# Four graph layers on one core: smaller diagonal tiles, one square per group and ten steps moved to ScalarE in the last layer

## The chip, the cores and the metric

The kernel runs on one core of one Trainium2 chip. The metric is device time in microseconds (us). The median of three runs of the kernel before is 1385.57 us, with 1384.66 us the lowest and 1387.64 us the highest. The engines are called by their names and by the short forms of the profile: TensorE (PE, with its weight loads PEld), VectorE (DVE), ScalarE (ACT), GpSimd (POOL) and SyncE (SP).

## The reference

The input is a matrix `x` of 4096 nodes by 64 features and a symmetric sparse adjacency matrix `adj` of 4096 by 4096. Four layers follow each other, each as `x = layernorm(x + layer(x, adj))`: a Chebyshev filter, a signed graph attention with a gated cell, a layer with decayed weights, and a hyperbolic layer. The change touches the last of them alone:

```python
def _mobius_add(x, y, c): ...
def _logmap(x, y, c):
    sub = _mobius_add(-x, y, c)
    sub_norm = jnp.maximum(jnp.linalg.norm(sub, axis=-1, keepdims=True), MIN_NORM)
    ...
    arg = jnp.clip(sqrt_c * sub_norm, 0.0, TANH_CLIP)
    return 2.0 / (sqrt_c * lam_x) * jnp.arctanh(arg) * sub / sub_norm

deg = jnp.maximum(adj.sum(axis=1, keepdims=True), 1e-08)
w = adj / deg
log_ij = _logmap(x[:, None, :], x[None, :, :], c)
agg = jnp.einsum('ij,ijc->ic', w, log_ij)
transformed = agg @ weight + bias
return _expmap(origin, transformed, c)
```

For each pair of nodes the kernel needs one scalar factor, an arctanh over its argument. It is a symmetric function of the pair, so the factor of a pair (i, j) serves (j, i) too. The kernel multiplies the adjacency matrix by the factors and then sums over the neighbours as matrix products.

## The kernel before, in words

The last layer goes over pairs of groups. A group is 512 nodes, four blocks of 128; there are eight groups, taken in the order `seq`. A tile is a pair of groups (i, j) with j not before i in `seq`: 36 tiles, in eight rows of 8, 7, 6, 5, 4, 3, 2 and 1 tiles. The first tile of each row is diagonal (i = j). A tile is worked on in two units of two blocks each, so there are 72 units; unit n belongs to tile n // 2, and `h` (0 or 1) is its half. An ordinary unit is 128 partitions by 2 x 512 = 1024 values. In a diagonal tile the first unit has the full 1024 values and the second unit only 2 x 256 = 512 (`columns`), because the lower left quarter of the tile is filled in by transposing the upper right one.

The chain of one unit is as follows.

- `product` (TensorE): two matrix products into the unit's PSUM tile `v_ps`. Unit n + 2 reuses the tile of unit n, so it waits for that unit's VectorE step at L1889.
- `square` (ScalarE, L1635): the square of the products, into `w3`.
- `opposite` (TensorE): a second pair of products added onto `v_ps`.
- `less_one` (VectorE, L1657): subtract a constant from the square and keep it above a floor (add, then max).
- ScalarE: logarithm of `w` (L1866), `exp(0.5 w)` into `rt` (L1867), `exp(-0.5 w)` (L1891), and later the logarithm of `rt` (L1900).
- VectorE: `rt = max(v, c) + rt` (L1889), and two units later the factor `f = min(rt, T_MAX) * w` (L1876) and `at = at * f` (L1879), the adjacency block times the factor.
- `turn` (TensorE transposes, L1678 and L1671): the factors of an off-diagonal tile are transposed for the mirrored tile, and VectorE multiplies the mirrored adjacency blocks (L1680, two per unit). In a diagonal tile four blocks are transposed and multiplied in (L1673), one iteration later than the factors themselves (`late_turns[n + 1]`).
- `gather` (TensorE, L1694 and L1706): the sums over the neighbours; ScalarE copies the mirrored part to `tb` (L1713).

The main loop runs one iteration per unit. The order of the main steps on ScalarE and on VectorE is fixed by hand: `behind(engine, ins)` ties each one to the one before it. In iteration n ScalarE does L1866(n), L1867(n), L1635(n + 1), L1891(n), a copy to `tb` in every second iteration, and L1900(n - 1). VectorE does L1876(n - 2), L1879(n - 2), L1889(n), L1657(n + 1), and two multiplications at L1680.

Other work is kept in a list of steps, `seam`; one step is taken at the end of each iteration. Its instructions are not tied, and the framework places them among the main ones. When a row of tiles is complete, six steps are added (`finals`): nothing, `first`, `second`, `third`, `fourth` and `fifth`, which turn the sums of a group into its output. `second` and `fourth` are mostly VectorE work, `third` takes the norm of each node with four squares on ScalarE that give their sums as well (L1808), followed by a maximum on VectorE (L1809) and small logarithms and exponentials on ScalarE (L1810 to L1812), and `fifth` is the layer norm. The last two groups are finished after the loop.

## Time and profile before

| what | value |
|---|---|
| median of three runs | 1385.57 us |
| profiled execution, its own time | 1386.67 us |
| its span, first to last instruction | 1384.9 us |
| granted TensorE clock, mean | 0.985 |
| PE busy | 1299.2 us (94%) |
| DVE busy | 1043.6 us (75%) |
| ACT busy | 810.5 us (59%) |
| first L1866 of the last layer | 958.62 us |
| last L1866 of the last layer | 1351.39 us |
| L1866, 128x1024, x64 from 880 us on | 1050 ns each |
| L1876, 128x1024, x64 from 880 us on | 1219 ns each |

The times come from one profiled execution. Its page gives the busy time of each engine, the span in 40 equal slices, and the costliest groups of instructions by source line. A group has the line, the engine, the operation, what it writes and reads, how often it ran, the busy time, the mean duration of one, and the idle time of the engine just before it with what ended that. "Busy" is an average over the four layers. The change is in the last layer, the last 430 us of the span, and it is read there.

### The profile page before, as it was taken

The page shows a single profiled execution, that of the slowest core. Times are in us where ns is not written, and L with a number is a line of the kernel's source. Part 1 is how long each engine was busy: PE and PEld are TensorE (multiplying, and loading weights), DVE is VectorE, ACT ScalarE, POOL GpSimd, SP SyncE. Part 2 cuts the span into 40 slices and gives each one's busy share as a digit, 9 for nine tenths or more (in the row PEclk, how much of TensorE's full clock was granted, in tenths as well). Part 3 has the DMA queues.
Part 4 walks back from the last instruction along what each step waited for, and adds up shares of the span by engine and source line. Part 5 has one row for each costly group of instructions (what it writes and reads, how often), then busy time and mean ns, then how long its engine had stood idle before and what let it go on. Part 6 is the DMA issues. An engine that isn't in the chain of part 4 may idle for free.

```text
span 1384.9 us, 19115 instructions
## 1 busy us (share of the span) xinstructions
PE 1299.2 (94%) x6812; PEld 613.3 (44%) x6812; DVE 1043.6 (75%) x1952; ACT 810.5 (59%) x1346; POOL 113.4 (8%) x200
## 2 busy tenths in 40 slices
PE   9999999999999999999999999998889898988984
PEld 6655656565544334444444323333334333433442
DVE  7789899899444257788885223335999999999997
ACT  5544444343000115654424775756989999999994
POOL 3111111101123000010111000001000000000000
PEclk9999999999999999999999999999999999999997
DMA  9999999999799999999985755443245453444430
GB/s 352 386 412 409 400 413 409 410 404 393 285 378 372 389 417 375 422 366 345 328 313 188 230 173 183 151 155 150 106 171 206 165 210 153 186 156 186 159 119 12
DMA packets 108191, 382.16 MB, mean 276 GB/s; under 512 B 20276, under 2 KB 20280, under 8 KB 76472
## 3 DMA queue, kind: packets, MB, share of 16 engines
q1 hardware_dynamic: 90472, 297.03, 57.8%
q0 software_dynamic: 12736, 76.29, 13.3%
q10 hardware_dynamic: 4880, 7.54, 1.4%
q8 instruction: 56, 0.92, 0.3%
q14 instruction: 47, 0.39, 0.1%
HBM read 294.05 MB, written 85.20 MB: 274 GB/s over the span
## 4 chain that ended last, share of the span: by engine, by line
PE 58%; ACT 17%; DVE 15%; DMA 6%; issue 3%; ACTq 0%; DVEq 0%; SPq 0%
PE pass L578 7%; PE tp L742 5%; PE w_ps L578 5%; DMA raw<-in_adj_dram 5%; PE cnt_ps L1506 4%; PE a_last L1215 4%; PE pass L571 4%; PE acc_ps L1466 4%; PE a_ps L1215 4%; ACT rt L1867 3%; ACT w L1866 3%; PE wide_last L1206 2%; DVE rt L1889 2%; ACT w L1635 2%; PE h_ps L571 2%
## 5 line engine op out<-in xcount | busy, mean ns | idle before, releaser
L749 ACT COPY at<-tp 128x512 f32<-128x512 f32 x248 | 127.9, 598 | 120.8 <-issue 91.2
L1511 ACT ACTIVATE wt<-cnt_ps 128x512 uint16<-128x512 f32 x212 | 117.4, 595 | 65.2 <-PE cnt_ps L1506 62.7
L777 DVE TENSOR_REDUCE dpart<-raw 128x4 f32<-128x2048 f32 x64 | 145.4, 2273 | 4.0 <-DMA raw<-in_adj_dram 3.8
L1694 PE MATMUL sums_ps<-at_d,some 128*64 128x512 f32 x288 | 143.8, 618 | 3.7 <-DVE at_d L1673 1.3
L779 DVE TENSOR_REDUCE lows<-raw 128x1 f32<-128x2048 f32 x64 | 145.4, 2272 | 0.0
L742 PE MATMUL tp<-ident,raw 128*128 128x128 f32 x1024 | 128.8, 279 | 9.1 <-DMA raw<-in_adj_dram 9.0
L742 PEld LDWEIGHTS tp<-ident,raw 128*128 128x128 f32 x1024 | 113.3, 142 | 45.0 <-issue 37.8
L1706 PE MATMUL sums_ps<-at_m,some 128*64 128x512 f32 x224 | 108.4, 605 | 0.2
L578 PE MATMUL pass<-at,cheb_n 128*128 128x512 f32 x224 | 97.5, 593 | 0.5 <-DVE cheb_n L811 0.5
L1623 PE MATMUL v_ps<-some,tr_a 64*128 64x512 f32 (+1 forms) x288 | 79.1, 626 | 17.9 <-DVE rt L1889 17.2
L578 PE MATMUL w_ps<-at,cheb_n 128*128 128x512 f32 x200 | 91.0, 598 | 0.0
L1889 DVE SCALAR_TENSOR_TENSOR rt<-v_ps,rt 128x1024 f32<-128x1024 f32 x72 | 83.4, 1158 | 6.7 <-ACT rt L1867 6.5
L1876 DVE SCALAR_TENSOR_TENSOR f<-rt,w 128x1024 f32<-128x1024 f32 x72 | 83.5, 1159 | 5.4 <-ACT rt L1900 5.2
L1506 PE MATMUL cnt_ps<-m,follow 128*64 128x512 fp8e4 x480 | 82.0, 391 | 4.7 <-ACT wt L1511 2.2
L1879 DVE TENSOR_TENSOR at_d<-at_d,f 128x1024 f32<-128x1024 f32 x72 | 83.7, 1163 | 1.2
L1866 ACT ACTIVATE w<-w 128x1024 f32<-128x1024 f32 x72 | 72.2, 1003 | 10.3 <-DVE w L1657 10.0
L1513 DVE TENSOR_SCALAR wt<-cnt_ps 128x512 uint16<-128x512 f32 x44 | 30.4, 692 | 61.8 <-PE cnt_ps L1506 61.8
L1867 ACT ACTIVATE rt<-w 128x1024 f32<-128x1024 f32 x72 | 72.8, 1010 | 2.0
L1680 DVE TENSOR_TENSOR at_m<-post,at_m 128x512 f32<-128x512 f32 x112 | 72.6, 684 | 0.1
L1900 ACT ACTIVATE rt<-rt 128x1024 f32<-128x1024 f32 x72 | 72.2, 1003 | 0.4
L1891 ACT ACTIVATE w<-w 128x1024 f32<-128x1024 f32 x72 | 72.1, 1002 | 0.0
L1678 PEld LDWEIGHTS post<-ident,f 128*128 128x128 f32 x448 | 47.6, 141 | 52.9 <-issue 34.6
(428 smaller groups left out, 2291.9 us busy)
## 6 DMA issues: line engine op xcount, KB each, us to landing
at<-adj_t SPq DMA_DIRECT2D x119, 1024.0 KB, 8.4
raw<-in_adj_dram SPq DMA_DIRECT2D x64, 1024.0 KB, 13.6
adj_t<-at POOLq DMA_DIRECT2D x62, 1024.0 KB, 8.1
at_d<-adj_t SPq DMA_DIRECT2D x36, 1024.0 KB, 4.6
at_m<-adj_t SPq DMA_DIRECT2D x28, 1024.0 KB, 6.7
m<-mask_t SPq DMA_DIRECT2D x120, 128.0 KB, 2.8
m<-mask_t SPq DMA_DIRECT2D x60, 256.0 KB, 3.5
mask_t<-mask ACTq DMA_DIRECT2D x28, 256.0 KB, 7.1
```

The costliest lines, as they stand in the source:

```text
L578: in_order(nc.tensor.matmul(ps, lhsT=cheb_n[:, jb, k : k + 2, :], rhs=rhs, start=first, stop=last))
L742: in_order(nc.tensor.transpose(tp[:, cols(b)], raw[:, b, cols(k)], ident))
L749: nc.scalar.copy(at[:, k, :], tp)
L777: in_order(nc.vector.tensor_reduce(dpart[:, g, c, :], raw, AX.X, ALU.add))
L779: in_order(nc.vector.tensor_reduce(lows[:, n : n + 1], raw.rearrange("p b j -> p (b j)"), AX.X, ALU.min))
L1215: in_order(nc.tensor.matmul(ps[q * F : (q + 1) * F, :], lhsT=nat_a[:, c * CB + k, 0:F], rhs=of[q if signed else 0][:, k, :], start=(c == 0 ...
L1506: in_order(nc.tensor.matmul(cnt[a][r * HP : (r + 1) * HP, :], lhsT=follow, rhs=chunks[c][odd][2 * a + r][:, k, :], start=(h == 2 * NB - 1) ...
L1511: in_order(nc.scalar.activation(wt[odd][a], cnt[a], AF.Relu, scale=-128.0))
L1694: in_order(nc.tensor.matmul(bank[0:F, :], lhsT=nat_c[:, j * CB + k, :], rhs=own[t][:, k, :], start=(i == j and k == 0), stop=(j == seq[-1] ...
L1866: behind("ACT", nc.scalar.activation(w, w, AF.Ln))
L1867: behind("ACT", nc.scalar.activation(rt, w, AF.Exp, scale=0.5))
L1889: behind("DVE", nc.vector.scalar_tensor_tensor(rt, vs[n][:, :, cs], (1.0 + V_FLOOR) * SCALE, rt, ALU.max, ALU.add))
```

## The change

The change has four parts.

First, a diagonal tile is cut to ten of its sixteen blocks of 128 x 128 where it was twelve. The first unit has 512 + 384 = 896 values, the second 256 + 128 = 384. `parts_of` gives the two pieces of a unit, `place` packs them without a gap in PSUM, and `flat` lets each ScalarE and VectorE step go over them as one run. The multiplication by the adjacency block (`at`) becomes two instructions in such a unit. Five blocks are transposed in the first unit and one in the second, where it was four for both; they are multiplied in by two instructions in the first unit and one in the second. They run in the same iteration as their factors (`late_turns[n]`), where it was one iteration later.

Second, `third` squares the whole group in one ScalarE instruction and sums it with one VectorE reduction.

Third, in some units `less_one` is a ScalarE instruction, a Relu with a bias from a tile, and the logarithm that follows gets the floor as a bias from the same tile. These are the units two after the iteration that takes a `second` or a `fourth` step.

Fourth, two constants for that are written to a new tile `shift` by GpSimd.

```diff
+        shift = op.tile([P, 2], F32, name="shift")
...
-        def columns(n):
+        def parts_of(n):
 
             i, j = tiles[n // 2]
-            return slice(2 * P if i == j and n % 2 else 0, GW)
+            if i != j:
+                return [(k, slice(0, GW), k * GW) for k in range(HB)]
+            if n % 2:
+                return [(0, slice(2 * P, GW), 2 * P), (1, slice(3 * P, GW), GW)]
+            return [(0, slice(0, GW), 0), (1, slice(P, GW), GW)]
+
+        def flat(t, n):
+
+            parts = parts_of(n)
+            k, cs, to = parts[-1]
+            return t.rearrange("p k i -> p (k i)")[:, parts[0][2] : to + cs.stop - cs.start]
...
+        by_scalar = set()
+        least = V_FLOOR * (V_FLOOR + 2.0) * SCALE**2
+
         def less_one(n):
             if n < NU:
-                w = ws[n][:, :, columns(n)]
+                w = flat(ws[n], n)
+                if n in by_scalar:
+                    behind("ACT", nc.scalar.activation(w, w, AF.Relu, bias=shift[:, 0:1]))
+                    return
                 ins = nc.vector.tensor_scalar(
-                    w, w, -SCALE * SCALE, V_FLOOR * (V_FLOOR + 2.0) * SCALE**2, ALU.add, ALU.max
+                    w, w, -SCALE * SCALE, least, ALU.add, ALU.max
                 )
...
             if i == j:
-                tp = ps_p.tile([P, GW], F32, name="post", tag="post")
-                for k in range(HB):
-                    for b in range(HB):
-                        nc.tensor.transpose(tp[:, cols(HB * k + b)], fs[t][:, b, cols(HB + k)], ident)
-                to = own[t][:, HB:CB, 0 : HB * P]
-                work.append(lambda: nc.vector.tensor_tensor(to, tp.rearrange("p (k i) -> p k i", k=HB), to, ALU.mult))
+
+                def mirror(blocks, to):
+                    tp = ps_p.tile([P, GW], F32, name="post", tag="post")
+                    for m, (b, k) in enumerate(blocks):
+                        nc.tensor.transpose(tp[:, cols(m)], fs[t][:, b, cols(k - b % HB)], ident)
+                    tp = tp[:, 0 : len(blocks) * P]
+                    if len(blocks) > 1:
+                        tp = tp.rearrange("p (k i) -> p k i", k=HB)
+                    work.append(lambda: nc.vector.tensor_tensor(to, tp, to, ALU.mult))
+
+                if h:
+                    mirror([(2, 3)], own[t][:, 3, cols(2)])
+                    return work
+                mirror([(0, 1)], own[t][:, 1, cols(0)])
+                mirror([(0, 2), (1, 2), (0, 3), (1, 3)], own[t][:, HB:CB, 0 : HB * P])
                 return work
...
                 sq = sm.tile([P, GB, F], F32, name="sqv", tag="t0")
-                for b in range(GB):
-                    nc.scalar.activation(sq[:, b, :], v[:, b, :], AF.Square, accum_out=n[:, b : b + 1])
+                nc.scalar.activation(sq, v, AF.Square)
+                nc.vector.tensor_reduce(n, sq, AX.X, ALU.add)
...
-                behind("ACT", nc.scalar.activation(w, w, AF.Ln))
+                behind("ACT", nc.scalar.activation(w, w, AF.Ln, bias=shift[:, 1:2] if n in by_scalar else 0.0))
...
-                behind("DVE", nc.vector.tensor_tensor(at, at, f, ALU.mult))
                 diagonal = tiles[t][0] == tiles[t][1]
+                if diagonal:
+                    for k, cs, to in parts_of(m):
+                        at = own[t][:, h * HB + k, cs]
+                        behind("DVE", nc.vector.tensor_tensor(
+                            at, at, f[:, k, to - k * GW : to - k * GW + cs.stop - cs.start], ALU.mult
+                        ))
+                else:
+                    at = own[t][:, hs, :]
+                    behind("DVE", nc.vector.tensor_tensor(at, at, f, ALU.mult))
...
-                if diagonal and h == 0:
-                    late_turns[n + 1] = (t, 0)
+                if diagonal:
+                    late_turns[n] = (t, h)
...
                 if seam:
-                    seam.pop(0)(ps_p)
+                    step = seam.pop(0)
+                    step(ps_p)
+                    if step in long_steps:
+                        by_scalar.add(n + 2)
```

More of the change, by code (lines that the diff above doesn't have):

```diff
@@ L1601, in load_mirrored @@
                 nc.sync.dma_start(mirrored[t], adj_t[j][:, i * CB : (i + 1) * CB, :])
-        def columns(n):
+        def parts_of(n):
             i, j = tiles[n // 2]
-            return slice(2 * P if i == j and n % 2 else 0, GW)
+            if i != j:
[7 more added lines that the diff above has]
+            return t.rearrange("p k i -> p (k i)")[:, parts[0][2] : to + cs.stop - cs.start]
+        nc.gpsimd.memset(shift[:, 0:1], -SCALE * SCALE * (1.0 + V_FLOOR * (V_FLOOR + 2.0)))
+        nc.gpsimd.memset(shift[:, 1:2], V_FLOOR * (V_FLOOR + 2.0) * SCALE**2)
         sums, fs = {}, {}
@@ L1611, in gnn4_kernel, with place @@
         NU = 2 * NT
+        def place(n, k, cs):
+            to = parts_of(n)[k][2] - k * GW
+            return vs[n][:, k, to : to + cs.stop - cs.start]
         def product(n):
@@ L1618, in product @@
             vs[n] = (ps_u if n % 2 else ps_v).tile([P, HB, GW], F32, name="v_ps")
-            cs = columns(n)
-            for k in range(HB):
+            for k, cs, _ in parts_of(n):
                 jb = j * CB + (n % 2) * HB + k
@@ L1623, in product @@
                 ins = nc.tensor.matmul(
-                    vs[n][:, k, cs], lhsT=tr_c[half, jb // 2, :], rhs=rights[i][0][half, cs], start=True, stop=True
+                    place(n, k, cs), lhsT=tr_c[half, jb // 2, :], rhs=rights[i][0][half, cs], start=True, stop=True
                 )
@@ L1633, in square @@
             ws[n] = wp3.tile([P, HB, GW], F32, name="w3")
-            cs = columns(n)
-            ins = nc.scalar.activation(ws[n][:, :, cs], vs[n][:, :, cs], AF.Square)
+            ins = nc.scalar.activation(flat(ws[n], n), flat(vs[n], n), AF.Square)
             behind("ACT", ins)
@@ L1641, in opposite @@
             i, j = tiles[n // 2]
-            cs = columns(n)
-            for k in range(HB):
+            for k, cs, _ in parts_of(n):
                 jb = j * CB + (n % 2) * HB + k
@@ L1646, in opposite @@
                 ins = nc.tensor.matmul(
-                    vs[n][:, k, cs], lhsT=tr_o[half, jb // 2, :], rhs=rights[i][1][half, cs],
+                    place(n, k, cs), lhsT=tr_o[half, jb // 2, :], rhs=rights[i][1][half, cs],
                     start=False, stop=True, skip_group_check=True,
@@ L1667, in turn @@
             if i == j:
-                tp = ps_p.tile([P, GW], F32, name="post", tag="post")
-                for k in range(HB):
-                    for b in range(HB):
-                        nc.tensor.transpose(tp[:, cols(HB * k + b)], fs[t][:, b, cols(HB + k)], ident)
-                to = own[t][:, HB:CB, 0 : HB * P]
-                work.append(lambda: nc.vector.tensor_tensor(to, tp.rearrange("p (k i) -> p k i", k=HB), to, ALU.mult))
+                def mirror(blocks, to):
[11 more added lines that the diff above has]
+                mirror([(0, 2), (1, 2), (0, 3), (1, 3)], own[t][:, HB:CB, 0 : HB * P])
                 return work
@@ L1744, in weights @@
                 nc.vector.tensor_copy(wh_x[half, q, :], spread_w[half, :])
-        turned_x, zs = {}, {}
+        turned_x, zs, long_steps = {}, {}, []
         def less_last(g):
@@ L1838, in fifth @@
                 nc.sync.dma_start(out[gcols(g), :].rearrange("(b p) f -> p b f", p=P), o_sb)
+            long_steps.extend([second, fourth])
             return [nothing, first, second, third, fourth, fifth]
@@ L1862, in gnn4_kernel @@
                     fs[n // 2] = fp.tile([P, CB, GW], F32, name="f3")
-                w, cs = ws[n][:, :, columns(n)], columns(n)
+                w = flat(ws[n], n)
                 rts[n] = el.tile([P, HB, GW], F32, name="rt3")
-                rt = rts[n][:, :, cs]
-                behind("ACT", nc.scalar.activation(w, w, AF.Ln))
+                rt = flat(rts[n], n)
+                behind("ACT", nc.scalar.activation(w, w, AF.Ln, bias=shift[:, 1:2] if n in by_scalar else 0.0))
                 behind("ACT", nc.scalar.activation(rt, w, AF.Exp, scale=0.5))
@@ L1872, in gnn4_kernel @@
                 t, h = divmod(m, 2)
-                cm = columns(m)
                 hs = slice(h * HB, (h + 1) * HB)
-                f, at = fs[t][:, hs, cm], own[t][:, hs, cm]
+                f = fs[t][:, hs, :]
                 behind("DVE", nc.vector.scalar_tensor_tensor(
-                    f, rts.pop(m)[:, :, cm], T_MAX, ws.pop(m)[:, :, cm], ALU.min, ALU.mult
+                    flat(f, m), flat(rts.pop(m), m), T_MAX, flat(ws.pop(m), m), ALU.min, ALU.mult
                 ))
-                behind("DVE", nc.vector.tensor_tensor(at, at, f, ALU.mult))
                 diagonal = tiles[t][0] == tiles[t][1]
+                if diagonal:
[7 more added lines that the diff above has]
+                    behind("DVE", nc.vector.tensor_tensor(at, at, f, ALU.mult))
                 before = t - 1 if t and tiles[t - 1][0] != tiles[t - 1][1] else None
                 gathers[n + 1] = (t, h, before)
-                if diagonal and h == 0:
-                    late_turns[n + 1] = (t, 0)
+                if diagonal:
+                    late_turns[n] = (t, h)
                 if not diagonal and h == 1:
@@ L1888, in gnn4_kernel @@
             if n < NU:
-                behind("DVE", nc.vector.scalar_tensor_tensor(rt, vs[n][:, :, cs], (1.0 + V_FLOOR) * SCALE, rt, ALU.max, ALU.add))
+                behind("DVE", nc.vector.scalar_tensor_tensor(rt, flat(vs[n], n), (1.0 + V_FLOOR) * SCALE, rt, ALU.max, ALU.add))
                 product(n + 2)
@@ L1898, in gnn4_kernel @@
             if 0 < n <= NU:
-                rt = rts[n - 1][:, :, columns(n - 1)]
+                rt = flat(rts[n - 1], n - 1)
                 behind("ACT", nc.scalar.activation(rt, rt, AF.Ln, scale=1.0 / SCALE))
```

## The prediction

> **What bounds the kernel now.** I read the page's slices first, then busy time by stretch, who waited for whom in that stretch, the groups by shape, and the timeline at row ends. The last layer begins at 958 us, the right third of the slices:

> ```profile
> DVE  7789899899444257788885223335999999999997
> ACT  5544444343000115654424775756989999999994
> ```

> Both engines are full there. From unit 18 to the loop's end:

> ```profile
> 1056.00:1352.00 296.00, 268.84 (x1283) 116.91 (x1284) 283.63 (x427) 289.97 (x418) 8.46 (x12) 0.99 0.44 166
> 1352.00:1385.00 33.00, 12.53 (x64) 6.30 (x62) 24.20 (x86) 15.47 (x65) 0.00 (x0) 0.78 0.06 12
> ```

> The columns are PE, PEld, DVE, ACT, POOL. ScalarE is busy 98% of those 296 us, VectorE 96%, TensorE 91%. Who waits in that stretch (us in total, times, longest):

> ```profile
> ACT w L1866 <- DVE w L1657: 2.7, 5, 0.9
> DVE f L1876 <- ACT rt L1900: 4.8, 11, 1.0
> DVE rt L1889 <- ACT rt L1867: 4.3, 7, 1.2
> ```

> ScalarE waits 2.7 us for `less_one`; VectorE waits 9.1 us for ScalarE. So ScalarE's own work is the nearer limit, and moving work to it is dear unless it lands on those 2.7 us. In steady units the two are close: successive L1866 are 4.97 us apart without a `tb` copy and 5.59 with one (1108.04, 1113.01, 1118.60, mean 5.28), successive L1876 5.33 (1108.17, 1113.50). What either gains alone, the other gives back.

> **Prices.** Count, busy, mean ns:

> ```profile
> L1866 ACT ACTIVATE w<-w 128x1024 f32<-128x1024 f32 x64 | 67.2, 1050 | 10.3 <-DVE w L1657 10.0
> L1866 ACT ACTIVATE w<-w 128x512 f32<-128x512 f32 x8 | 5.0, 621 | 0.0
> L1876 DVE SCALAR_TENSOR_TENSOR f<-rt,w 128x1024 f32<-128x1024 f32 x64 | 78.0, 1219 | 5.4 <-ACT rt L1900 5.2
> L1876 DVE SCALAR_TENSOR_TENSOR f<-rt,w 128x512 f32<-128x512 f32 x8 | 5.5, 684 | 0.0
> L1657 DVE TENSOR_SCALAR w<-w 128x1024 f32<-128x1024 f32 x64 | 44.0, 688 | 1.6 <-ACT w L1635 1.4
> L1657 DVE TENSOR_SCALAR w<-w 128x512 f32<-128x512 f32 x8 | 3.3, 418 | 0.0
> L1812 ACT ACTIVATE vn<-nv,ln_two 128x4 f32<-128x4 f32 x8 | 2.3, 284 | 0.0
> L1811 ACT ACTIVATE vn<-nv 128x4 f32<-128x4 f32 x8 | 1.6, 198 | 0.1
> ```

> A block's 128 columns cost ScalarE (1050 - 621) / 4 = 107 ns per step and VectorE (1219 - 684) / 4 = 134 ns, or 67 ns at `less_one`. A bias read from a tile costs 284 - 198 = 86 ns. Neighbours overlap by 0.08 to 0.1 us, so 1050 ns takes 0.95 us of ScalarE and 688 ns takes 0.60 of VectorE.

> **Part 1, smaller diagonal tiles.** Sixteen units lose 128 columns in five ScalarE steps: 0.535 us a unit, 1.07 a tile, 8.6 in all. VectorE loses 3 x 134 + 67 = 469 ns a unit and gains a second `at` (0.07 of start-up) and a one-block product (128 columns, 0.20): net -0.20 a unit. The four-block product (L1673) moves one iteration earlier, into the heavier first one, behind `less_one`, so it delays no `less_one` of its own iteration; the 0.18 to 0.61 us that VectorE waited for its transposes goes. TensorE gets two transposes more a tile (0.13 each by L1671's spacing) and narrower products; it had 27 us to spare in the stretch. The next `gather` is queued behind the new one-block product, 0.2 us later, with the next opposite product behind it, which is early by over a microsecond: nothing, or those 0.2 us per tile (1.6) if that cover goes.

> What of the 1.07 arrives? In rows 1 to 3 ScalarE is already ahead of VectorE at a diagonal tile and waits for it:

> ```profile
> 1197.46 1.05 ACT L1900 ACTIVATE rt<-rt 128x1024 f32<-128x1024 f32 x1
> 1198.83 1.06 ACT L1866 ACTIVATE w<-w 128x1024 f32<-128x1024 f32 x1 [0.31 <-DVE w L1657]
> ```

> There only VectorE's part of the path shortens: two `less_one` and two L1889, 0.40 us a tile. The rest becomes a longer wait at L1866. In the last rows no such wait precedes the tile, and most of the 1.07 counts.

> **Part 2, one square per group.** Four squares and four sums occupy 0.96 us:

> ```profile
> 1153.81 1.05 ACT L1900 ACTIVATE rt<-rt 128x1024 f32<-128x1024 f32 x1
> 1154.75 0.24 ACT L1808 ACTIVATE sqv<-v 128x64 f32<-128x64 f32 x1
> ...
> 1155.62 0.19 ACT L1808 ACTIVATION_READ_ACCUMULATOR sqv<-v 128x1 f32 x1
> 1155.71 1.04 ACT L1866 ACTIVATE w<-w 128x1024 f32<-128x1024 f32 x1
> 1156.65 0.19 ACT L1810 ACTIVATE nv<-nv 128x4 f32<-128x4 f32 x1
> ```

> One 128x256 instruction takes 0.37 (L1765), 0.30 of the engine: -0.67 a group. VectorE's reduction (L1789, same shape, 411 ns) adds 0.33. It lies between ScalarE's square and its next small logarithm, L1810, and there it adds a wait. After L1900 ends, ScalarE would reach L1810 after 0.30 + 0.95 = 1.25 us. VectorE, released by the same L1900, does L1876 (1.15), the reduction (0.33), the maximum and the handover (0.2): 1.7. So L1810 waits 0.45, and L1867, L1635 and VectorE's L1889 queue behind it. Net -0.22 a group; -0.67 if the framework puts L1810 later. In the tail the same trade is within 0.3 either way.

> **Part 3, `less_one` on ScalarE.** A row's last gather is issued in iteration 2 x (last tile) + 4, `second` two later, `fourth` four later. The marked units are 22, 24, 36, 38, 48, 50, 58, 60, 66 and 68; later ones fall outside the loop. No Relu of this shape is in the trace. Lower bound 0.95 (as L1866), upper 1.14 (1050 + 86, no overlap); I take 0.95 + 0.08 = 1.03, and 0.09 for the bias of the following logarithm: 1.12 a unit, against 0.60 saved on VectorE.

> The Relu runs one iteration after the long VectorE step, in ScalarE's iteration of `third` (unit n + 2 of `second`) or `fifth`. It stands ahead of L1900, and VectorE's L1876 waits for that. At 1154.88 and 1158.59 VectorE waits for ScalarE already (0.21 and 1.22), so the 0.60 saved there is idle time. After `fourth` VectorE is late too, but the two tie: L1866 of unit 39 starts at 1172.70 with ScalarE's last instruction just done. Taking 0.60 from VectorE leaves ScalarE the late one.

> [...]

> **The sum.** Row 1's end, from L1866 of unit 32 (1132.92) to that of unit 44 (1198.83), was 65.91 us: ScalarE's path to unit 41 (1184.60), VectorE's from there (L1876 at 1184.72 and 1195.12). ScalarE's piece changes by 1.12 - 0.22 (after `second`), + 1.12 (after `fourth`), - 0.11 (L1900 of the cut unit 31): +1.9. VectorE's changes by -0.40. Row net: +1.5.

> - Rows 0 and 1: +1.5 each.
> - Row 2: ScalarE idled 0.41 at unit 51 behind `less_one`; that fills: +1.0.
> - Row 3: units 58 and 60, the latter cut (-0.12), with part of its diagonal on ScalarE's path: +1.2.
> - Row 4: 0.68 of idle at unit 68 fills and the diagonal's 1.07 counts whole: -0.1.
> - Tile 0: 1.07 less for ScalarE at the start, where VectorE (L1876 at 966.95) waits for it; then VectorE's layer-2 remnants bound: -0.6. Tile 8: -0.4.
> - Last two diagonals and the tail's gather: -1.2.

> 1.5 + 1.5 + 1.0 + 1.2 - 0.1 - 0.6 - 0.4 - 1.2 = +2.9 us. The profiled execution took 1386.67 us, 1384.9 of it span; it becomes 1389.6. It stood 1.1 above the median of 1385.57, so the median becomes 1388.5.

> **Rivals.**
> *The row ends are VectorE's* (faster). If VectorE's long steps set ScalarE's start there, Relu fills gaps. ScalarE's ledger from unit 18: ten Relus 10 x 1.12 - 0.2 = +11.0, six diagonal tiles -6.4, five squares -3.3: +1.3. If all its idle goes too (2.7 seen, perhaps 1 too short to be listed), that is -2.4; with the start, tile 8 and the tail -1.6: -4.0, 1381.6. It decides once the waits at L1866 after `second` and `fourth` reach 1.1 us a unit; for it speaks that parts 1 and 2 lighten ScalarE, against it that those waits total 1.1 us (units 51 and 68).
> *The waits add up* (much slower). No idle fills (+1.1), the gathers' 0.2 a tile shows (+1.6), Relus cost 1.14 (+1.1): +6.7, 1392.3. VectorE's 9.1 us of waits speak for it, TensorE's room against it.
> *A table load at each Relu* would add 10 x 2 x 1.283 = 26 us. Against it: Relu (L1511, until 953.5) and logarithms (L298, from 864.7) alternate after the last load at 808.9. I give it none.

> **How the numbers follow.** Forecast 0.55: its own range is +1 to +5 us, so 0.30 of it lies above +2.8 us (0.2%, about what a measurement of this kernel can tell from no change) and 0.25 within. Faster rival 0.27: 0.22 beyond -2.8, 0.05 within. Much slower 0.18. Slower 0.30 + 0.18 = 0.48, same 0.25 + 0.05 = 0.30, faster 0.22. The range runs from the faster rival's 1382 to the slower one's 1392.

> **What would show it.** Right: ScalarE at 99% from 1056 us on, VectorE under 95%, VectorE's waits at L1876 and L1889 above 9.1 us, L1866 at diagonal units waiting about 0.6 longer, ten Relus near 1135 ns, L1810 with a wait for L1809. Wrong: VectorE's waits falling, or L1866 of units 23 to 25 and 37 to 39 starting earlier after their row's diagonal than before.

## The result and the profile after

The changed kernel took 1390.51 us (median of 7 runs, 1388.96 to 1392.75) against 1385.57 us (7 runs as well): a ratio of 1.0033 with a 95% interval of 1.0023 to 1.0042. Twelve later runs gave 1.0024 (1.0014 to 1.0035). It is slower by about 4 us. The profiled execution took 1391.5 us, 1389.7 of it span, 4.8 more than before.

The same views as in the prediction follow, of the changed kernel. The slices:

```profile
DVE  7789999899343267888885224346999999988987
ACT  5554444443000115754424775646899999999993
PEclk9999999999999999999999999999999999999998
```

VectorE reads 8 in three of its last five slices, where it read 9 before; ScalarE stays at 9 up to the last slice. Busy time by stretch (PE, PEld, DVE, ACT, POOL, then the granted clock; the last two columns are the DMA share and GB/s):

```profile
1352.00:1385.00 33.00, 16.82 (x84) 8.63 (x82) 27.70 (x97) 14.81 (x44) 0.65 (x2) 0.87 0.03 6
1056.00:1352.00 296.00, 268.97 (x1275) 115.38 (x1273) 272.50 (x440) 287.15 (x389) 7.82 (x10) 0.97 0.44 166
```

VectorE went from 283.63 to 272.50 us busy, ScalarE from 289.97 to 287.15 (97%), and the mean clock from 0.99 to 0.97. The waits in 1056 to 1352 us (total, times, longest):

```profile
ACT w L1897 <- DVE w L1678: 3.9, 5, 1.3
ACT w L1651 <- PE v_ps L1640: 1.9, 2, 1.7
DVE f L1906 <- ACT rt L1938: 12.2, 10, 2.8
DVE at_m L1710 <- PE post L1708: 3.5, 3, 1.8
DVE rt L1927 <- ACT rt L1898: 3.2, 3, 1.8
DVE at_d L1697 <- PE post L1693: 2.1, 5, 0.6
```

L1897, L1906 and L1927 are the former L1866, L1876 and L1889. VectorE's wait for ScalarE grew from 9.1 to 15.4 us. Waits for TensorE grew too, on both engines: at L1651, the square, from 0.2 us; at L1710, the product with a transposed tile, from nothing listed; and at L1697, the diagonal's product, from 1.0 us (there the prediction had expected the waits to go).

The prices, by shape (count, total, mean ns):

```profile
L1676 ACT ACTIVATE w<-w,shift 128x1024 f32<-128x1024 f32 x8 | 9.1, 1138 | 0.0
L1897 ACT ACTIVATE w<-w,shift 128x1024 f32<-128x1024 f32 x8 | 9.1, 1136 | 0.0
L1897 ACT ACTIVATE w<-w 128x896 f32<-128x896 f32 x6 | 5.7, 942 | 0.9 <-DVE w L1678 0.9
L1897 ACT ACTIVATE w<-w 128x384 f32<-128x384 f32 x8 | 4.1, 517 | 0.0
```

The Relu and the logarithm with a bias take 1138 and 1136 ns, which is 1050 + 86 as priced; 128 columns less take 108 and 104 ns off a step (1050 to 942, 621 to 517).

One row end, in order of time (start, duration, engine):

```profile
1153.48 1.14 ACT L1676 ACTIVATE w<-w,shift 128x1024 f32<-128x1024 f32 x1
1154.52 1.04 ACT L1938 ACTIVATE rt<-rt 128x1024 f32<-128x1024 f32 x1
1155.47 0.40 ACT L1837 ACTIVATE sqv<-v 128x256 f32<-128x256 f32 x1
1155.60 1.22 DVE L1906 SCALAR_TENSOR_TENSOR f<-rt,w 128x1024 f32<-128x1024 f32 x1 [1.83 <-ACT rt L1938]
1155.78 1.13 ACT L1897 ACTIVATE w<-w,shift 128x1024 f32<-128x1024 f32 x1
...
1158.20 0.16 DVE L1839 TENSOR_SCALAR nv<-nv 128x4 f32<-128x4 f32 x1
1158.24 1.01 ACT L1651 ACTIVATE w<-v_ps 128x1024 f32<-128x1024 f32 x1
...
1159.14 0.20 ACT L1840 ACTIVATE nv<-nv 128x4 f32<-128x4 f32 x1
```

The Relu stands ahead of L1938 and VectorE waits 1.83 us, where it waited 0.21: that chain is as predicted. The small logarithm (L1840, the former L1810) is not as predicted. The framework put it behind L1651, and it waits for nothing.

The following table is made from such timelines: the time between the starts of marked steps, each minus the same stretch before, so that the layers ahead do not count: between executions they moved the start of the last layer from 956.06 to 962.07 us. Units are numbered by their L1897 (the same logarithm in kernels with other line numbers); the end is the start of the last copies to `o_sb`. The ratios are to runs of the kernel before beside them (medians of 1385.57 in the first row of ratios, 1386.7 to 1387.4 in the others). Each row is one execution, the ratio is of many: the two executions of the changed kernel differ by 0.49 us in the second column and 1.07 in the third, and the one of the Relus alone, at 1395.82 us, was slower than its median of 1393.9.

| kernel | unit 0 to 18 | 18 to 68 | 68 to 71 | 71 to the end | sum | ratio of the times (95%) |
|---|---|---|---|---|---|---|
| before, us | 97.86 | 276.73 | 18.18 | 28.85 | 421.62 | |
| changed | -1.09 | +2.72 | +1.71 | +1.59 | +4.93 | 1.0033 (1.0023 to 1.0042) |
| changed, again | -1.06 | +3.21 | +0.64 | +1.59 | +4.38 | 1.0024 (1.0014 to 1.0035) |
| no Relu | -1.05 | -5.02 | +3.44 | +1.60 | -1.03 | 0.9984 (0.9969 to 0.9998) |
| Relus alone | 0.00 | +10.67 | +0.15 | +0.07 | +10.89 | 1.0056 (1.0038 to 1.0075) |
| one square alone | +0.01 | -2.81 | +0.48 | +0.61 | -1.71 | 0.9983 (0.9972 to 0.9993) |
| diagonal alone | -1.05 | -1.93 | +0.20 | +1.06 | -1.72 | 0.9991 (0.9981 to 1.0001) |
| Relus behind `second` | -1.05 | +0.39 | +0.34 | +3.29 | +2.97 | 1.0019 (1.0005 to 1.0033) |
| Relus behind `fourth` | -1.06 | -3.63 | 0.00 | +1.60 | -3.09 | 0.9983 (0.9971 to 0.9995) |
| changed, filled | -1.06 | +2.28 | -0.09 | +1.60 | +2.73 | 1.0024 (1.0011 to 1.0037) |
| changed, filled, again | -1.06 | +2.23 | -0.09 | +1.59 | +2.67 | 1.0023 (1.0011 to 1.0034) |
| no Relu, filled | -1.06 | -4.18 | +0.20 | +1.60 | -3.44 | 0.9965 (0.9953 to 0.9977) |
| no Relu, end as before | -1.06 | -5.08 | +0.61 | -0.30 | -5.83 | 0.9957 (0.9943 to 0.9971) |
| the same, filled | -1.06 | -4.14 | +0.53 | -0.29 | -4.96 | 0.9954 (0.9940 to 0.9968) |

### The profile page after: what moved, and what is told of

The parts are those of the page before. It is cut to its first block, busy times and chain, and to the rows that moved or that the text cites. A ratio compares the mean times of both kernels' runs of the same rounds, so it can differ in the third digit from the quotient of the medians.

```text
span 1389.7 us, 19135 instructions
## 1 busy us (share of the span) xinstructions
PE 1305.2 (94%) x6828; PEld 616.4 (44%) x6828; DVE 1036.4 (75%) x1982; ACT 807.3 (58%) x1300; POOL 112.7 (8%) x202
## 4 chain that ended last, share of the span: by engine, by line
PE 57%; ACT 17%; DVE 13%; DMA 8%; issue 4%; ACTq 0%; DVEq 0%; SPq 0%
PE pass L578 7%; DMA raw<-in_adj_dram 6%; PE w_ps L578 6%; PE tp L742 6%; PE cnt_ps L1506 4%; PE a_last L1215 4%; PE pass L571 4%; PE acc_ps L1466 4%; PE a_ps L1215 4%; ACT rt L1898 3%; ACT w L1897 3%; PE wide_last L1206 2%; ACT w L1651 2%; ACT w L1929 2%; ACT wt L1511 2%
## 5 line engine op out<-in xcount | busy, mean ns | idle before, releaser
L1511 ACT ACTIVATE wt<-cnt_ps 128x512 uint16<-128x512 f32 x212 | 117.4, 595 | 65.2 <-PE cnt_ps L1506 62.9
L1724 PE MATMUL sums_ps<-at_d,some 128*64 128x512 f32 x288 | 150.6, 641 | 1.8 <-DVE at_d L1918 1.1
L1640 PE MATMUL v_ps<-some,tr_a 64*128 64x512 f32 (+3 forms) x288 | 79.0, 614 | 15.5 <-DVE rt L1927 14.9
L1906 DVE SCALAR_TENSOR_TENSOR f<-rt,w 128x1024 f32<-128x1024 f32 (+1 forms) x72 | 81.2, 1128 | 12.5 <-ACT rt L1938 12.3
L1927 DVE SCALAR_TENSOR_TENSOR rt<-v_ps,rt 128x1024 f32<-128x1024 f32 (+1 forms) x72 | 81.2, 1127 | 5.3 <-ACT rt L1898 5.2
L1710 DVE TENSOR_TENSOR at_m<-post,at_m 128x512 f32<-128x512 f32 x112 | 72.5, 680 | 4.7 <-PE post L1708 4.7
L1898 ACT ACTIVATE rt<-w 128x1024 f32<-128x1024 f32 (+1 forms) x72 | 71.0, 986 | 2.0
L1938 ACT ACTIVATE rt<-rt 128x1024 f32<-128x1024 f32 (+1 forms) x72 | 70.6, 980 | 0.7 <-DVE rt L1927 0.2
L1929 ACT ACTIVATE w<-w 128x1024 f32<-128x1024 f32 (+1 forms) x72 | 70.4, 978 | 0.0
L571 PE MATMUL h_ps<-at,cheb_n 128*64 128x512 f32 x288 | 69.4, 603 | 0.0
L1651 ACT ACTIVATE w<-v_ps 128x1024 f32<-128x1024 f32 (+1 forms) x72 | 67.8, 941 | 2.6 <-PE v_ps L1640 2.2
```

Source lines behind the costliest of these rows:

```text
L571: in_order(nc.tensor.matmul(ps[q * F : (q + 1) * F, :], lhsT=cheb_n[:, jb, k, :], rhs=rhs, start=first, stop=last, skip_group_check=True,))
L1511: in_order(nc.scalar.activation(wt[odd][a], cnt[a], AF.Relu, scale=-128.0))
L1724: in_order(nc.tensor.matmul(bank[0:F, :], lhsT=nat_c[:, j * CB + k, :], rhs=own[t][:, k, :], start=(i == j and k == 0), stop=(j == seq[-1] ...
L1898: behind("ACT", nc.scalar.activation(rt, w, AF.Exp, scale=0.5))
```

## Experiments

My theory was that of the prediction: the Relus cost their full time on ScalarE's path and parts 1 and 2 give little back. The rivals were that the row ends belong to VectorE, and that something else (TensorE, the transposes) makes the loss.

**One part at a time.** The Relus taken out of the changed kernel:

```diff
-                    if step in long_steps:
-                        by_scalar.add(n + 2)
```

> The change without the ten moves to ScalarE (less_one stays on VectorE everywhere). Theory (ScalarE's queue bounds the loop, and each Relu with its biased logarithm is paid there, about 0.9 to 1.1 us each): 7 to 10 us less than the changed kernel, so 2 to 5 us less than before; the last L1897 about 5 us earlier than before, the stretch behind the loop about 1.5 us longer as in the changed kernel. Rival (the loss comes from the diagonal's earlier transposes and the longer tail, the Relus lie in gaps): still at least 2 us above before.

1384.0 us, 0.9984. From unit 18 to 68 parts 1 and 2 gain 5.02 us. Between units 68 and 71, 3.44 us are lost again, and 1.60 behind the loop. The waits from 1324 to 1352 us name the place:

```profile
ACT xw L1795 <- PE post L1789: 4.1, 1, 4.1
DVE at_m L1710 <- PE post L1708: 3.8, 1, 3.8
```

Both engines stand still for TensorE (L1795 copies a product that the work behind the loop needs). The part on the end of the loop returns to that.

The Relus alone, in the kernel before, with the tile `shift` and the biased logarithm as in the change (not printed here):

```diff
+                if n in by_scalar:
+                    behind("ACT", nc.scalar.activation(w, w, AF.Relu, bias=shift[:, 0:1]))
+                    return
...
+                    if step in long_steps:
+                        by_scalar.add(n + 2)
```

> The kernel before with the ten moves to ScalarE alone. Theory: +8 to +11 us over before, nearly all of it in steps of about 2 us at each of five row ends, the tail unchanged. Rival (Relus in gaps): +0 to +3 us.

1393.9 us, 1.0056. From unit 18 to 68 it loses 10.67 us for ten Relus, 1.07 each, and 2.09, 1.94, 2.24 and 4.40 us by the rows of the table further down, which hold two, two, two and four: with nothing else changed they all stand on the path.

One square alone, in the kernel before:

```diff
-                for b in range(GB):
-                    nc.scalar.activation(sq[:, b, :], v[:, b, :], AF.Square, accum_out=n[:, b : b + 1])
+                nc.scalar.activation(sq, v, AF.Square)
+                nc.vector.tensor_reduce(n, sq, AX.X, ALU.add)
```

> The kernel before with one square and one reduction per group alone. Theory: ScalarE's 0.67 us a group is mostly given back to the wait for VectorE's reduction: within 1 us of before in the loop; behind the loop the three reductions add up to 1 us to VectorE. Total -1 to +1 us. Rival (ScalarE's saving counts whole in the loop): -3 us.

1385.17 us, 0.9983. It gains 2.81 us by unit 68, 0.56 for each of five groups: nearly the whole saving of ScalarE, as the rival said, with no wait at the small logarithm. Behind the loop it loses 0.61.

The diagonal tiles alone (the changed kernel without Relus and with the four squares):

```diff
-                nc.scalar.activation(sq, v, AF.Square)
-                nc.vector.tensor_reduce(n, sq, AX.X, ALU.add)
+                for b in range(GB):
+                    nc.scalar.activation(sq[:, b, :], v[:, b, :], AF.Square, accum_out=n[:, b : b + 1])
-                    if step in long_steps:
-                        by_scalar.add(n + 2)
```

> The kernel before with the smaller diagonal tiles alone. Theory: the loop ends 4 to 5 us earlier; the tail gives back about 0.5 to 1.5 us because the last tile's transposes come one iteration earlier and wait for a free PSUM tile: -3 to -4.5 us. Rival (the earlier transposes stall TensorE in the loop too): 0 to +2 us.

1385.35 us, 0.9991. It gains 1.05 at the first diagonal and at tile 8, then 0.51 or 0.52 in each of rows 0 to 2, 0.38 between units 54 and 68, nothing from there to unit 71, and loses 1.06 behind the loop. I had looked for 3 us or more.

**Which Relus cost.** Only those behind `second`, then only those behind `fourth`:

```diff
-            long_steps.extend([second, fourth])
+            long_steps.extend([second])
```

> The changed kernel with the Relus kept only behind `second` (units 22, 36, 48, 58, 66); behind `fourth` less_one is VectorE's again. Theory (each Relu costs ScalarE about 1.1 us on the path, the two of a row end alike): half of what all ten cost, so about 3.5 us below the changed kernel, 1387, a ratio near 1.001 to the kernel before. Rival (the Relu behind `fourth` relieves a VectorE that is late there, so the ones behind `second` cost all): no more than 1 us below the changed kernel, 1389.5 or more, ratio 1.003.

```diff
-            long_steps.extend([second, fourth])
+            long_steps.extend([fourth])
```

> The changed kernel with the Relus kept only behind `fourth` (units 24, 38, 50, 60, 68). Theory (both places cost alike): 1387, ratio near 1.001. Rival (those behind `second` cost all): 1384 to 1384.5, the same as without any Relu, ratio 0.998 to 0.999. In the starts of L1897 the step of a row end shows it: with the theory about 1 us later at units 24, 38, 50 than without any Relu, with the rival nothing.

1389.74 us (1.0019) and 1384.26 us (0.9983): the kernel with the Relus behind `fourth` is as fast as the one with none. That comparison flatters them, for the kernel with none lost 3.44 us between units 68 and 71, for another reason (below), and this one nothing. From unit 18 to 68 the five Relus behind `fourth` cost 1.39 us and the five behind `second` 5.41. By rows, in us against the kernel without Relus:

| units | before | no Relu against before | behind `second` adds | behind `fourth` adds | changed against before |
|---|---|---|---|---|---|
| 18 to 32 | 76.44 | -1.02 | +1.11 | +0.92 | +1.01 |
| 32 to 44 | 65.91 | -1.14 | +1.13 | +0.78 | +0.77 |
| 44 to 54 | 55.58 | -0.96 | +1.12 | +0.17 | +0.34 |
| 54 to 68 | 78.80 | -1.90 | +2.05 (two Relus) | -0.48 (two Relus) | +0.60 |

Behind `second` each Relu costs 1.03 to 1.13 us, the 1.12 of the sum. Behind `fourth` it costs most of that in the first two rows and next to nothing in the later ones. There it falls into time in which ScalarE waited: between units 44 and 54 ScalarE's idle time falls from 1.73 to 1.04 us, between 54 and 68 from 2.94 to 1.02, while in the first two rows it stays (1.79 and 1.78, 1.61 and 1.51). So neither theory held whole: the same instruction is nearly free in one place and costs all in the other. In the first three rows the kernel without Relus and the two additions make up the changed kernel. In the last they do not (-0.33 against +0.60, and +1.06 in its other execution); with TensorE filled, as below, that row stands at -0.07. VectorE's wait at L1906, 3.3 us without Relus, tells the two places apart. From 1056 to 1352 us, behind `second`:

```profile
DVE f L1906 <- ACT rt L1938: 11.4, 8, 2.8
```

and behind `fourth`:

```profile
DVE f L1906 <- ACT rt L1938: 4.6, 10, 1.2
```

**The end of the loop.** In the changed kernel TensorE stands idle while it waits for a late square, and then runs at half its clock. Slices of one microsecond (columns as above, so the clock is third from the right):

```profile
1326.00:1327.00 1.00, 0.42 (x1) 0.09 (x1) 1.00 (x2) 0.97 (x2) 0.00 (x0) 1.00 0.00 0
1327.00:1328.00 1.00, 0.00 (x0) 0.00 (x0) 1.00 (x2) 1.00 (x2) 0.00 (x0) 1.00 0.66 147
1328.00:1329.00 1.00, 0.27 (x2) 0.09 (x1) 1.00 (x3) 1.00 (x4) 0.00 (x0) 0.89 0.95 369
1329.00:1330.00 1.00, 0.63 (x2) 0.51 (x4) 1.00 (x3) 1.00 (x4) 0.00 (x0) 0.50 1.00 426
...
1335.00:1336.00 1.00, 1.00 (x4) 0.09 (x1) 0.05 (x1) 0.97 (x2) 0.00 (x0) 0.69 0.03 8
1336.00:1337.00 1.00, 1.00 (x7) 0.52 (x6) 0.12 (x1) 0.93 (x1) 0.00 (x0) 1.00 0.00 0
```

The timeline shows who is late for it:

```profile
1328.17 0.27 PE L1661 MATMUL v_ps<-wq_signed,some 64*128 64x256 bf16 x2 [1.75 <-ACT w L1651]
1329.37 2.08 PE L1640 MATMUL v_ps<-some,tr_a 64*128 64x512 f32 x4 [0.93 <-DVE rt L1927]
...
1336.88 0.69 DVE L1710 TENSOR_TENSOR at_m<-post,at_m 128x512 f32<-128x512 f32 x1 [1.83 <-PE post L1708]
...
1338.64 1.02 ACT L1651 ACTIVATE w<-v_ps 128x1024 f32<-128x1024 f32 x1 [1.71 <-PE v_ps L1640]
```

Four products take 2.08 us (1.13 at 1337.47, at full clock), then VectorE and ScalarE wait 1.83 and 1.71 us. To test it I gave TensorE more work and nothing else: three iterations behind each `third` do their turning transposes twice.

```diff
-                for k in range(CB):
-                    nc.tensor.transpose(tp[:, cols(k)], fs[t][:, k, cols(b)], ident)
+                for _ in range(2 if again else 1):
+                    for k in range(CB):
+                        nc.tensor.transpose(tp[:, cols(k)], fs[t][:, k, cols(b)], ident)
...
+                    if step in third_steps:
+                        refilled.update(n + d for d in range(1, 4))
```

> The changed kernel with more work for TensorE and nothing else: in the three iterations behind each `third` the turning transposes are done twice into the same bank (about 1 us of TensorE each). In the changed kernel the granted clock falls to about half for 2 to 4 us after waits of 1.7 us of TensorE for the late square (1171, 1241, 1328 us), and the products and transposes behind it are late. Theory (the idle gaps bring the slow clock, and it costs 1.5 us at units 68 to 70): the dips at 1171, 1241 and 1328 go, the clock rises from 0.982 to 0.985 or more, time 1 to 2 us below the changed kernel (1388.5 to 1389.5). Rival (the dips come by themselves or cost nothing; VectorE and ScalarE set the end): the same time as the changed kernel or up to 2 us more, for the added transposes delay the real ones by up to 0.5 us each.

> The changed kernel once more, unaltered, to stand beside the same kernel with filled idle time on the same chip: ratio 1.003 to the kernel before.

> The changed kernel with the turning transposes done twice behind each `third`, once more. Theory (half clock costs the changed kernel 1.5 to 2 us at units 68 to 70, as its first profile says): ratio 1.002, 1.2 to 2 us below the changed kernel of the same call. Rival (chance between executions): the two within 0.5 us.

> The changed kernel without Relus, with the same filling. Without it the clock stood at 0.50 from 1334.9 to 1341.7 us, and ScalarE waited 4.05 us behind it; L1897 lost 3.5 us between units 70 and 71. Theory (that loss is the slow clock's, brought by TensorE's idle 1331 to 1333): L1897 of unit 71 as early as that of unit 70 against the kernel before (-6), time 1380.5 to 1382, ratio 0.9955 to 0.9965. Rival (the extra transposes of the last two diagonals for a full `post` make the loss): -2.5 at unit 71 again, 1384, ratio 0.998.

In all filled kernels the slow stretches are gone: no slice of 5 us from 1056 to 1351 us has a clock below 0.95, where the changed kernel had five stretches at half clock. Without Relus the stretch that had stood at 0.50 reads

```profile
1321.00:1333.00 12.00, 11.55 (x61) 5.46 (x59) 12.00 (x32) 10.30 (x16) 0.00 (x0) 1.00 0.34 123
1333.00:1343.00 10.00, 9.99 (x61) 5.77 (x61) 8.89 (x15) 9.12 (x16) 0.00 (x0) 1.00 0.08 16
```

Units 68 to 71 fall from +1.71 and +0.64 to -0.09 in the changed kernel (both times), and from +3.44 to +0.20 without Relus. That the slow clock follows from the idle time, and that it made the loss between units 68 and 71, is shown by this. It does not cost wherever it stands: the stretch at 1171.8 us of the changed kernel is missing in its other execution, and the row took 66.68 and 66.69 us. The filling has a price too: where no slow stretch held anybody up, units 18 to 68 took 0.84 us longer with it (-5.02 and -4.18, without Relus).

What it is worth in time is less sure. Without Relus the filled kernel took 1382.46 us and the ratio fell from 0.9984 to 0.9965, in two sets of runs whose intervals overlap. The changed kernel took 1390.74 us when first filled, where 1388.5 to 1389.5 was expected; later 1391.01 unfilled and 1389.71 us filled, from the same set of runs, with ratios of 1.0024 and 1.0023, do not tell the two apart.

**The tail, and a faster kernel.** Behind the loop the changed kernel loses 1.59 us, in both executions, and 1.59 or 1.60 filled. (With the Relus behind `second` it was 3.29; in that execution the clock stood at half from 1358.0 to 1361.4 us, and the small logarithm waited 4.65 us where it waits 2.96 below.) The timeline of the tail:

```profile
1360.76 0.66 PE L1693 MATMUL post<-ident,f 128*128 128x128 f32 x4 [1.07 <-DVE at_m L1710]
...
1365.81 1.29 DVE L1710 TENSOR_TENSOR at_m<-post,at_m 128x512 f32<-128x512 f32 x2 [1.22 <-PE post L1708]
...
1367.86 0.20 ACT L1840 ACTIVATE nv<-nv 128x4 f32<-128x4 f32 x1 [2.96 <-DVE nv L1839]
```

The last diagonal tile's transposes, now an iteration earlier, wait for a free `post`; all queued behind them on TensorE is late; and the norm waits for VectorE's reduction. If so, the last tile and the last three groups should keep the old form. That kernel has parts 1 and 2 elsewhere, and no Relu:

```diff
+        whole = {NT - 1}
...
+                if t in whole:
+                    mirror([(0, 2), (1, 2), (0, 3), (1, 3)], own[t][:, HB:CB, 0 : HB * P])
+                    return work
...
-                nc.scalar.activation(sq, v, AF.Square)
-                nc.vector.tensor_reduce(n, sq, AX.X, ALU.add)
+                if g in seq[-3:]:
+                    for b in range(GB):
+                        nc.scalar.activation(sq[:, b, :], v[:, b, :], AF.Square, accum_out=n[:, b : b + 1])
+                else:
+                    nc.scalar.activation(sq, v, AF.Square)
+                    nc.vector.tensor_reduce(n, sq, AX.X, ALU.add)
...
-                    if step in long_steps:
-                        by_scalar.add(n + 2)
```

> Smaller diagonal tiles except the last one (left as before, its four-block transposes one iteration later, as before), one square only for the five groups finished inside the loop and the four squares for the three groups behind it, no Relu. Theory (parts 1 and 2 gain about 2.8 us each in the loop, and what the tail gives back, 0.6 to 1.6 us, comes from the last tile's extra transposes and the three late reductions): 4 to 6 us below the kernel before, 1380 to 1381.5, ratio 0.996 to 0.997; tail from L1897 of unit 71 to the last o_sb as long as before (28.85 us). Rival (the slow clock after TensorE's waits and VectorE's bound eat it as in the run without Relu): 1384, ratio 0.998, tail 1 to 2 us longer.

> The kernel with the last diagonal tile and the last three groups as before and no Relu, with the same filling. Its one stretch at half clock (1320.5 to 1324) held up nobody, so the theory says no gain: within 1 us of the unfilled one, ratio 0.9955 to 0.9965. Rival (half clock costs wherever it stands): 1 to 2 us less, ratio 0.994 to 0.995.

1380.73 us, 0.9957 (0.9943 to 0.9971): faster than both kernels. The tail gives 0.30 back where it took 1.60; the diagonal tile and the squares were put back together, so their shares are those of the single parts (1.06 and 0.61). The filled one, 1381.62 us and 0.9954, is no better, as expected: the one slow stretch of the unfilled kernel (1320.6 to 1324.0 us, shown below) delayed nobody. With it units 18 to 68 gain 5.08 us; the kernel without Relus, which has none there, gains 5.02.

## Why the prediction was right or wrong

The direction was right (slower), and so was the mechanism for the Relus behind `second`; 1390.51 us lies between the forecast's 1388.5 and the upper end of 1392. The sum of the profiled execution was +2.9 and came to +4.93 (again +4.38). That it came so near is in part luck: up to unit 68 the sum was 2.4 us too high (again 1.9), and behind it 4.5 us too low (again 3.4).

- *Tile 0 and tile 8*, -0.6 and -0.4: the loop's start to unit 18 measured -1.09. Right.
- *Part 1 in rows 0 to 2*: -0.40 of VectorE's and -0.11 of ScalarE's path is -0.51 a row; alone it measured -0.51, -0.52 and -0.52. Right.
- *Part 1 in rows 3 and 4*: a part of one diagonal and the whole 1.07 of another were counted; alone units 54 to 68 gained 0.38. VectorE's waits for the diagonal's transposes, which were to go, moved to the new one-block product and grew from 1.0 to 2.1 us.
- *Part 2, the wait of 0.45 at L1810*: wrong. The prediction's own alternative came true (the framework puts L1810 later), and the square is worth -0.56 a group instead of -0.22. That is five times 0.34, or 1.7 us.
- *Part 3 behind `second`*: 1.12 predicted, 1.03 to 1.13 measured. Right, and so was the reason, that the 0.60 saved is VectorE's idle time.
- *Part 3 behind `fourth`*: 1.12 predicted; 0.92, 0.78, 0.17 and -0.48 measured. The tie that the prediction read at unit 39 held in the first two rows. In the later ones ScalarE had time to fill, which was the mechanism of the faster rival; the prediction allowed for such filling at two units alone, 51 (0.41) and 68 (0.68).
- So units 18 to 68, in which all ten Relus lie, cost +2.72 (again +3.21), where the five rows were to cost 1.5 + 1.5 + 1.0 + 1.2 - 0.1 = +5.1.
- *The last two diagonals and the tail*, -1.2: from unit 68 on, +3.30 was measured (1.71 + 1.59; again 0.64 + 1.59 = +2.23). This is the step that failed most. The 1.07 us of ScalarE did not count whole in the last tiles (alone: +0.20 from unit 68 to 71), the transposes that were said to cost nothing wait for a `post` tile, three reductions late in the tail cost 0.61 where 0.3 was allowed, and the clock was not considered at all, since the row of before had it at 0.99. That mean hid two stretches at half clock in the kernel before (3.4 us each, from 1083.8 and 1281.7 us).

Of the signs that were named, VectorE under 95% (92%), its waits above 9.1 us (15.4), Relus near 1135 ns (1138) and longer waits at diagonal units came as said: L1897 of units 32 and 44 waits 0.96 and 0.87 us, 0.55 more than before. ScalarE at 99% did not come (97%), nor the wait at L1810 within the loop. Of the signs of being wrong none came: units 23 to 25 and 37 to 39 start 0.05 to 1.24 us later after the first unit of their row (16 and 30) than before.

At 128x1024 the Relu takes 1138 ns on ScalarE, VectorE's step 683 ns. The five Relus behind `second` cost 5.41 us in all; the five behind `fourth`, at the same 1138 ns, cost 1.39 us: 1.70 in the first two rows, of which 0.31 came back in the later ones. The place decides, more than the rate. Without any Relu the kernel stands at 0.9984, about 2 us faster than the one before, and about 6 us only with the end left as before.

## What to carry to other kernels

When two engines alternate on the path, cost a moved instruction place by place: the same Relu cost its full 1.1 us where the saved time was VectorE's idle time, and 0.17 us or less where ScalarE itself had been waiting. Leave the last iterations in the form that keeps their queues short: the steps that gained in the loop lost 1.6 us behind it. When a change makes TensorE wait in a few places, read the granted clock in slices of a microsecond, not its mean.

## What the runs showed of the hardware

Around the slow stretch of the changed kernel, from 1327 to 1337 us, the granted clock was either full or 0.50 of it: every slice of 0.1 us reads 1.00 or 0.50, but for the two in which it changes (0.93 and 0.94). From 1056 us to the loop's end the changed kernel has five slow stretches and the kernel before two; each began 0.19 to 1.96 us after the end of a wait of TensorE that had lasted 1.29 to 2.17 us. In the kernel with the old end and no Relu:

```profile
1318.00:1319.00 1.00, 0.28 (x3) 0.17 (x2) 1.00 (x1) 1.00 (x3) 0.00 (x0) 1.00 0.00 0
1319.00:1320.00 1.00, 0.19 (x2) 0.02 (x1) 1.00 (x3) 1.00 (x3) 0.00 (x0) 1.00 0.88 139
1320.00:1321.00 1.00, 0.78 (x4) 0.30 (x4) 1.00 (x4) 1.00 (x4) 0.00 (x0) 0.80 0.87 352
1321.00:1322.00 1.00, 1.00 (x6) 0.10 (x4) 1.00 (x4) 0.97 (x4) 0.00 (x0) 0.50 1.02 434
...
1324.00:1325.00 1.00, 1.00 (x5) 0.27 (x2) 1.00 (x5) 0.28 (x1) 0.00 (x0) 1.00 0.00 0
```

TensorE is busy 0.47 of two microseconds, and the clock then stands at 0.50 from 1320.6 (0.80 is 0.6 of full and 0.4 of half) to 1324.0, for 3.4 us. In the changed kernel 0.69 of three microseconds were busy and the slow stretch lasted 6.8 us, from 1328.8 to 1335.6, twice as long. A similar gap need not bring it: in the kernel before TensorE waited 1.85 us until 1225.97 and 2.17 us until 1327.04, and the next 10 us had the clock at 1.00.

In the 3.41 us ahead of each of the seven starts TensorE was busy for 1.32 to 1.72 us. In steps of 3.413 us counted on from 1281.74, the gap until 1327.04 was split over two steps, with 2.17 and 2.27 us busy. The other gap lay in one step, counted from either start, with 1.56 us busy, and brought nothing. So 1.56 us went without a slow stretch where 1.67 and 1.72 us, in the changed kernel, had one behind them: these two profiles show no sharp limit. Waits of 1.29 to 2.17 us were enough for a slow stretch, and waits of 1.85 and 2.17 us also went without one.
